# The entry of a last 3x3 convolution: where a row buffer lies, who fills it, and when the other path's result is added

## The chip, the cores and the metric

The kernel runs on one core of one Trainium2 chip. The metric is the device time in microseconds (us) of one execution. The engines of the core run at the same time, each through its own instructions in order: TensorE (PE) multiplies matrices, VectorE (DVE) and ScalarE (ACT) work on elements, GpSimd (POOL) and SyncE (SP) here mostly issue transfers (DMA). A transfer issued by an engine stands in that engine's order too: if it has to wait for a buffer, all that is behind it on that engine waits as well.

## The reference

Four layers work on an array of 4 images, 256 channels, 64 x 64 pixels. Each layer normalises its input over groups of 8 channels, computes a branch and adds the branch to its input. The branches are an axial attention, a ternary 3x3 convolution, a binary network with two 3x3 convolutions, and a plain 3x3 convolution. The change sits between the third and the fourth.

```
x = x + attention(group_norm(x))
x = x + ternary_conv(group_norm(x))
x = x + binary_net(group_norm(x))       # ends with batch_norm(leaky_relu(conv)) on half of the channels
x = x + conv3x3(group_norm(x), W) + bias
```

In the third branch, the last batch normalisation needs sums over all four images before one of its values can be scaled. Its input is called y here (128 channels for each image), and the scaled result is added to the first 128 channels of x. The fourth layer's group normalisation needs x with that addition.

## The kernel before

All four layers are in one program. The chip's memory next to the engines (SBUF) has 128 partitions; a tile holds one channel in each. Tiles come from pools, and pools that are opened one after the other lie one behind the other in memory. When a stage is closed, the next stage's pools are laid over the same bytes; a tile of the new stage can be written only when the last reader of the bytes below it is done. So the order in which pools are opened decides which work of the old stage a new buffer waits for. The binary network's stage opens the pools `e_x`, `e_p`, `e_j`, `e_s`, `e_x1`, ... from the low end. `e_x` (three buffers) and `e_x1` (one) hold input rows, `e_p` a padded input, `e_j` values that nobody reads, and `e_s` the sums and small vectors, which are in use to the stage's very end. The last convolution's stage opens its pools in the order of a string, "t3 m r01 y t0 c s r10 r11 p0 t1 o t2 r00 u0 p1 u1".

A scheduler orders the instructions of each engine at compile time, by priorities that follow the program's order. `tc.high_priority()` puts a block ahead, and `tc.issue_after(i)` places instructions on the engine of `i` behind it. Once made, the orders are fixed.

The last convolution works by image b, by half t of its 256 input channels, by upper and lower half h of the image, and by half co of the output channels. Its steps, with the lines of the profile:

- `fetch` (L1253): a load on SP of 33 rows of x from the output array `out` into the buffer `r` with t and h in its name.
- `measure` (L1267, L1268): on ScalarE, sum and sum of squares of those rows. `norm` then does a chain of small operations, with a square root on ScalarE (L106).
- `transform`: ScalarE normalises the 33 rows into a padded buffer, `g_pad` (L1321, called the fill). VectorE then forms linear combinations of the rows (L1073 to L1086, 12 operations, into `gtr` and `gtm`) and of the columns (L1095, 4 operations, into `gtc`).
- `chunk(b, h, co)`: TensorE makes nine tiles of products, numbered 0 to 8 (L1113, L1120), in a ring of seven PSUM buffers. For tiles 1, 4 and 6 ScalarE makes two copies (L1137, L1138) out of PSUM, and VectorE goes on with them (L1140, L1144, ... L1179). A PSUM buffer is free for a later tile only then. The result `gc_o` is added into `out` by an accumulating transfer on POOL (L1182); for the last image's lower half the sum is made on VectorE and stored by SP (L1186, L1187).

The third layer's result reaches the fourth in two ways. For image 0, upper channels (t = 0), `first_y` adds the scaled y to the fetched rows on VectorE (L1306, ten operations), with the squares on ScalarE (L1316), as soon as the batch normalisation's scale is known. For all images, `add_y` adds it to `out` itself in four pieces. One piece, called a pass here, is a load of y on SP (L1294, into one of two buffers `gy`), a scaling on ScalarE (L1295) and an accumulating transfer on POOL (L1296). Image 1's passes come first, then those of images 0, 2 and 3, at places that `rest` writes down. `fetch` of an image's t = 0 rows has to wait for the passes of the same pixels.

For image 0, `chunk` begins with the t = 1 products of seven tiles, so that TensorE has work while t = 0 is still being made ready.

Of the kernel before, what the change touches and what calls it, by code (L numbers as in the profile page):

```python
# [12 lines left out]
AF = mybir.ActivationFunctionType  # L13
ALU = mybir.AluOpType
# [5 lines left out]
B = 4  # L20
# [21 lines left out]
def network(ctx: ExitStack, tc, x, wqkv, relm, relt, relw, relv, counts, masks, vecs, rowv, ab, w1, l2w1, l2w2, l3w, mats, out):  # L42
# [725 lines left out]
    def from_scores(general, keep):  # L768
# [331 lines left out]
        def output_rows(ring, cp, op, uw, vs, co, res, out_, bias, name, order):  # L1100


            ms, copies = {}, []

            def product(i, t, first, last):
                k, cs = TILES[i]
                if first:
                    ms[i] = ring.tile([P, 8, 64], F32, name=f"{name}_{i}", tag="conv")
                u1, u2 = uw[t]
                v1, v2 = vs[t]  # L1110
                if cs is None:
                    for dx in range(3):
                        nc.tensor.matmul(  # L1113
                            ms[i], lhsT=u1[:, dx, k // 2, bass.ts(co, P)], rhs=v1[:, k // 2, :, dx : dx + 64],
                            start=(first and dx == 0), stop=(last and dx == 2),
                        )
                else:
                    m = ms[i].rearrange("p q (a w) -> p (q a w)", a=2).rearrange("p (a n) -> p a n", a=2)
                    for a, c in enumerate(cs):
                        nc.tensor.matmul(  # L1120
                            m[:, a], lhsT=u2[:, c, k // 2, bass.ts(co, P)],
                            rhs=v2[:, c, k // 2].rearrange("p q w -> p (q w)"), start=first and a == 0, stop=last and a == 1,
                        )

            def tile_(tag):
                return (cp if tag == "c0" else op).tile([P, 512], F32, name=f"{name}_{tag}", tag=tag)

            def halves(a):
                return a.rearrange("p (a n) -> p a n", a=2)

            def flat(m):
                return m.rearrange("p q w -> p (q w)")

            def columns(i, copied, scratch_):
                pair = halves(flat(ms[i]))
                c2 = halves(copied)
                copies.append(nc.scalar.copy(c2[:, 0], pair[:, 1]).ins)  # L1137
                nc.scalar.mul(c2[:, 1], pair[:, 1], -1.0)  # L1138
                sd = halves(scratch_)
                nc.vector.tensor_tensor(sd, pair[:, 0:1].to_broadcast([P, 2, 256]), c2, ALU.add)  # L1140
                return sd

            def whole(i, sd, dst):
                nc.vector.tensor_tensor(  # L1144
                    dst.rearrange("p (n a) -> p a n", a=2), halves(flat(ms[i])), sd, ALU.add
                )

            o4 = op.tile([P, 8, 4, 64], F32, name=f"{name}_o", tag="o4")
            c0, s0, c1, s1 = (tile_(tag) for tag in ("c0", "s0", "c1", "s1"))
            begun = order[2] if order else 0  # L1150
            if order:
                for i in range(begun):
                    product(i, order[0], True, False)
            for i in range(len(TILES)):
                if i < begun:
                    product(i, order[1], False, True)
                else:
                    product(i, 0, True, False)
                    product(i, 1, False, True)
                c, sm = (c0, s0) if i < 3 else (c1, s1)  # L1160
                if i in (1, 4, 6):
                    sd = columns(i, c, sm)
                elif i in (2, 5, 7):
                    whole(i, sd, c)
                if i == 2:
                    m1 = flat(ms[0])
                    nc.vector.scalar_tensor_tensor(s0, m1, bias, c0, ALU.add, ALU.add)
                    nc.vector.scalar_tensor_tensor(c0, m1, bias, c0, ALU.add, ALU.subtract)
                elif i == 5:
                    m3 = flat(ms[3])  # L1170
                    nc.vector.tensor_tensor(s1, m3, c1, ALU.add)
                    nc.vector.tensor_tensor(c1, m3, c1, ALU.subtract)
                    nc.vector.scalar_tensor_tensor(o4[:, :, 2, :], as_rows(s1), 4.0, as_rows(s0), ALU.mult, ALU.add)
                    nc.vector.tensor_tensor(s0, s0, s1, ALU.add)
                    nc.vector.scalar_tensor_tensor(o4[:, :, 1, :], as_rows(c1), 2.0, as_rows(c0), ALU.mult, ALU.add)
                    nc.vector.scalar_tensor_tensor(c0, c1, 8.0, c0, ALU.mult, ALU.add)
                elif i == 7:
                    nc.vector.tensor_tensor(o4[:, :, 0, :], as_rows(c1), as_rows(s0), ALU.add)
            nc.vector.tensor_tensor(o4[:, :, 3, :], ms[8], as_rows(c0), ALU.add)  # L1179
            of = o4.rearrange("p q r w -> p (q r w)")  # L1180
            if res is None:
                nc.gpsimd.dma_start(out=out_, in_=of, accum_op=ALU.add)  # L1182
            else:
                for half in range(2):
                    cols = bass.ts(half, HW // 4)
                    nc.vector.tensor_tensor(of[:, cols], of[:, cols], res[:, cols], ALU.add)  # L1186
                    nc.sync.dma_start(out=out_[:, cols], in_=of[:, cols])  # L1187
            return copies[0]

        def as_rows(a):  # L1190
            return a.rearrange("p (q w) -> p q w", w=64)
# [16 lines left out]
        def conv_layer(name, ph, layout, own, biases, first):  # L1208
# [78 lines left out]
                        nc.vector.tensor_tensor(nb, nb, rs[:, i : i + 1], ALU.mult)  # L1287
                    norms[b, t] = nb, rs[:, i : i + 1]

            def add_y(b, src, scale, shift):  # L1290
                for k in range(4):
                    cols = bass.ts(k, HW // 4)
                    yk = ps_["y"].tile([P, HW // 4], F32, name=f"{name}y_{b}_{k}", tag="y")
                    nc.sync.dma_start(out=yk, in_=src[b][:, cols])  # L1294
                    nc.scalar.activation(yk, yk, AF.Identity, bias=shift, scale=scale)  # L1295
                    nc.gpsimd.dma_start(out=out[b, 0:P, cols], in_=yk, accum_op=ALU.add)  # L1296
# [21 lines left out]
            def transform(b, t, h, pinned=False):  # L1318

                nb, rs = norms[b, t]  # L1320
                filled[b, t, h] = nc.scalar.activation(  # L1321
                    pads[h][:, 1 - h : 34 - h, 1:65], raws[b, t, h], AF.Identity, bias=nb, scale=rs
                ).ins
                v1 = ps_[f"t{2 * h + t}"].tile([P, 3, 8, 66], F32, name=f"{name}tr_{b}_{t}_{h}", tag="tr")
                v2 = ps_[f"t{2 * h + t}"].tile([P, 4, 3, 8, 32], F32, name=f"{name}tc_{b}_{t}_{h}", tag="tc")
                m = ps_["m"].tile([P, 3, 8, 66], F32, name=f"{name}tm_{b}_{t}_{h}", tag="tm")
                input_rows([(v1 if k % 2 else m)[:, k // 2] for k in range(6)], pads[h], pinned)
                ready[b, t, h] = input_columns(v2, m).ins
                vs[b, t, h] = v1, v2
# [8 lines left out]
            def rest(later):  # L1338
                for b in range(B):
                    more = b + 1 < B  # L1340
                    if b > 0:
                        transform(b, 0, 1)
                    chunk(b, 0, 0, first if b == 0 else None)
                    if b > 0:
                        transform(b, 1, 1)
                    if more:
# [3 lines left out]
                        with tc.issue_after(filled[b, 0, 1]):  # L1350
                            measure(b + 1, 1, 0)
                            if b > 0:
                                measure(b + 1, 0, 0)
                    copy = chunk(b, 0, 1, None)
                    if more:
                        for t in (1, 0):
                            fetch(b + 1, t, 1)
# [2 lines left out]
                        with tc.issue_after(copy if b == 0 else filled[b, 0, 1]):  # L1360
                            if b == 0:
                                measure(b + 1, 0, 0)
                            measure(b + 1, 0, 1)
                            if b == 0:
                                later(0)
                        norm(b + 1, slice(0, 2))
                        transform(b + 1, 0, 0)
                    copy = chunk(b, 1, 0, None)
                    if more:
                        transform(b + 1, 1, 0)  # L1370
                        if b + 2 < B:
                            with tc.issue_after(copy):
                                later(b + 2)
                    chunk(b, 1, 1, None)

            return set_up, load_weights, fetch, measure, norm, load_y, first_y, add_y, transform, rest, filled, got, ready

# [255 lines left out]
        with ExitStack() as ph:  # L1633
            xp3 = pool(ph, "e_x", 3)
            padp = pool(ph, "e_p")
            jp = pool(ph, "e_j")
            sp = pool(ph, "e_s")
            xp1 = pool(ph, "e_x1")
            lp = pool(ph, "e_l")
            yps = {b: pool(ph, f"e_y{b}") for b in (3, 0, 1, 2)}  # L1640
            wp2 = pool(ph, "e_w2")
# [237 lines left out]
        with ExitStack() as ph:  # L1879
# [10 lines left out]
            set_up(0)  # L1890
            load_weights(1, nc.gpsimd)
            transform(0, 1, 0)
            for h in range(2):
                fetch(0, 0, h)
            load_y(y_d)
            with tc.high_priority():
                first_y(sy2)
# [2 lines left out]
                norm(0, slice(0, 1), cy2)  # L1900
                transform(0, 0, 0)
            with tc.issue_after(filled[0, 0, 0]), tc.issue_after(got[0, 0, 0]):
                add_y(1, y_d, sy2, cy2)
            with tc.issue_after(ready[0, 1, 0]):
                set_up(1)
            with tc.issue_after(ends[3, 3]):
                transform(0, 1, 1, True)
            transform(0, 0, 1, True)
            rest(lambda b: add_y(b, y_d, sy2, cy2))
        return lost  # L1910

    lost = from_scores(False, keep)
# [114 lines left out]
```

## Time and profile before

| | us |
|---|---|
| median of 3 runs (lowest to highest) | 2702.37 (2691.62 to 2704.37) |
| profiled execution | 2695.66 |
| its span, from the first to the last instruction | 2693.9 |
| busy in the span: TensorE | 2323.6 (86%) |
| busy in the span: VectorE | 1977.6 (73%) |
| busy in the span: ScalarE | 1299.7 (48%) |
| busy in the span: GpSimd | 167.8 (6%) |

Busy shares are averages over four very different layers. The last convolution takes only the last 470 us of the span, from 2222 us on, and the change touches its first stretch. Times in the text are from the start of the span, so that every row can be found on the same axis. In a timeline row the first number is the start, the second the duration, and the brackets at the end give the idle time of that engine just before the row and what ended it.

### The profile page before, as it was taken

What the parts mean: (1) busy time and instruction counts of PE and PEld (TensorE: products, weight loads), DVE (VectorE), ACT (ScalarE), POOL (GpSimd) and SP (SyncE); (2) the same over time, 40 slices, a digit from 0 to 9 for tenths busy, and PEclk for the clock granted to TensorE, in tenths of its full rate; (3) what the DMA queues carried; (4) which work ended last, traced back from release to release, by engine and by line L of the source; (5) the groups of instructions that cost most, each with busy time, mean ns of one, the idle gap of its engine ahead of it and who ended that gap; (6) DMA issues with size and microseconds to landing.
All of it is one profiled execution on the core that took longest, in us unless ns stands there. A gap on an engine that the chain in (4) does not pass through costs nothing. (4 is left out here: it accounts for less than half of the span.)

```text
span 2693.9 us, 78726 instructions
## 1 busy us (share of the span) xinstructions
PE 2323.6 (86%) x34816; PEld 1620.9 (60%) x34816; DVE 1977.6 (73%) x3326; ACT 1299.7 (48%) x2114; POOL 167.8 (6%) x285
## 2 busy tenths in 40 slices
PE   7999888888998788878884999998887887899998
PEld 4656655556666566667663777776444444566665
DVE  6766787888876466666667989986677787688884
ACT  3556354555555654454434655553445753433210
POOL 0000100000000100000000011111000010100000
PEclk9999899999999789989896999999988997999999
DMA  6866476667666887777777666525655775746221
GB/s 234 269 194 196 127 196 183 169 155 202 177 156 146 251 276 252 255 245 257 249 237 255 225 206 226 181 110 193 160 152 170 237 263 150 160 108 148 42 47 49
DMA packets 284832, 505.64 MB, mean 188 GB/s; under 512 B 32896, under 2 KB 149248, under 8 KB 270784
## 3 DMA queue, kind: packets, MB, share of 16 engines
q1 hardware_dynamic: 214336, 347.46, 42.3%
q0 software_dynamic: 21888, 94.32, 13.8%
q10 hardware_dynamic: 48256, 58.73, 6.2%
q8 instruction: 275, 4.51, 0.7%
q14 instruction: 77, 0.63, 0.1%
HBM read 270.45 MB, written 229.97 MB: 186 GB/s over the span
## 5 line engine op out<-in xcount | busy, mean ns | idle before, releaser
L515 DVE STREAM_TRANSPOSE t<-pd 128x1024 f32<-128x1024 f32 x256 | 304.4, 1227 | 84.0 <-PE pd L508 83.1
L508 PE MATMUL pd<-rm,qb 64*32 64x256 f32 x8192 | 310.7, 390 | 48.8 <-DVE t L515 34.6
L1613 PE MATMUL pc<-e_tr,e_k 128*64 128x512 bf16 x2304 | 273.7, 399 | 59.5 <-DVE e_tr L1602 27.9
L535 ACT ACTIVATE o<-pq 128x512 f32<-128x512 f32 x256 | 150.5, 593 | 280.6 <-PE pq L529 280.6
L1113 PE MATMUL gc<-gtr,g_u 128*128 128x512 f32 x576 | 262.6, 608 | 12.8 <-DVE gtr L1077 5.4
L1613 PEld LDWEIGHTS <-e_k 128*64 128x64 bf16 x2304 | 155.6, 114 | 175.6 <-issue 73.9
L508 PEld LDWEIGHTS pd<-rm,qb 64*32 64x32 f32 x8192 | 171.5, 108 | 143.9 <-DVE t L515 60.5
L1509 PE MATMUL dc<-dh,d_u 128*128 128x512 f32 x768 | 230.9, 412 | 23.8 <-ACT dh L1486 21.1
L940 ACT ACTIVATE pt<-pt,sm 128x512 f32<-128x512 f32 x256 | 162.3, 709 | 167.6 <-DVE pt L910 167.6
L1509 PE MATMUL dc<-dl,d_u 128*128 128x512 f32 x768 | 226.5, 405 | 0.9 <-DVE dl L1487 0.7
L1113 PEld LDWEIGHTS gc<-gtr,g_u 128*128 128x128 f32 x576 | 111.2, 195 | 139.2 <-issue 121.3
L529 PEld LDWEIGHTS pq<-t,t 64*64 64x64 f32 x8192 | 143.8, 136 | 83.9 <-issue 74.7
L529 PE MATMUL pq<-t,t 64*64 64x64 f32 x8192 | 165.4, 224 | 26.9 <-issue 25.4
L1120 PE MATMUL gc<-gtc,g_u 128*128 128x256 f32 x768 | 177.5, 388 | 11.3 <-DVE gc_s L1140 7.3
L1509 PEld LDWEIGHTS dc<-dh,d_u 128*128 128x128 f32 x768 | 147.3, 193 | 64.5 <-ACT dh L1486 22.6
L1120 PEld LDWEIGHTS gc<-gtc,g_u 128*128 128x128 f32 x768 | 148.6, 194 | 49.3 <-issue 13.7
L1509 PEld LDWEIGHTS dc<-dl,d_u 128*128 128x128 f32 x768 | 144.8, 190 | 41.9 <-DVE dl L1487 3.4
L910 DVE TENSOR_TENSOR pt<-e_False,si_False 128x1024 f32<-128x1024 f32 x123 | 145.6, 1214 | 25.8 <-PE e_False L898 22.2
L898 PE MATMUL e_False<-qc_False,rw 32*128 32x256 f32 x984 | 124.1, 462 | 31.8 <-DVE pt L910 15.5
L541 ACT ACTIVATE sq<-o 128x1024 bf16<-128x1024 f32 x128 | 135.3, 1057 | 3.9
L291 PE MATMUL po<-xg,wt 128*128 128x512 f32 x256 | 121.0, 612 | 5.3 <-DVE st L298 3.7
L1003 PE MATMUL pe_False<-pt,ve 128*32 128x64 f32 x4096 | 90.8, 243 | 37.9 <-issue 33.1
(415 smaller groups left out, 3913.3 us busy)
## 6 DMA issues: line engine op xcount, KB each, us to landing
si_False<-qk_d SPq DMA_DIRECT2D x64, 1024.0 KB
qk_d<-o SPq DMA_DIRECT2D x496, 128.0 KB
x<-x_d SPq DMA_DIRECT2D x32, 1056.0 KB
gr<-out SPq DMA_DIRECT2D x16, 1056.0 KB
xa<-in_x SPq DMA_DIRECT2D x16, 1024.0 KB
vt_d<-vs ACTq DMA_DIRECT2D x32, 512.0 KB
q_d<-qs SPq DMA_DIRECT2D x64, 256.0 KB
qb<-q_d SPq DMA_DIRECT2D x128, 128.0 KB
```

Source lines behind the costliest of these rows:

```text
L508: nc.tensor.matmul(pds[t][32 * c : 32 * c + 32, m].rearrange("p j k -> p (j k)"), lhsT=q[rows, 2 * (gp % 2) + g, a, 32 * nb : 32 * nb + 32 ...
L515: nc.vector.transpose(ts[t][:, :, 32 * jh : 32 * jh + 32].rearrange("p a j b -> p j a b"), pds[t].rearrange("p m j k -> p j m k"),)
L529: nc.tensor.matmul(ps[nb][64 * g : 64 * g + 64, m, :], lhsT=ts[1][rows, n // 2, :, n % 2], rhs=ts[0][rows, n // 2, :, n % 2], start=True, ...
L535: nc.scalar.activation(o[:, :, n : n + 8, :], ps[nb].rearrange("p n (a b) -> p a n b", b=2), AF.Copy, accum_out=acc[:, nb, gp, col : col + 1],
L541: nc.scalar.activation(junk, part, AF.Square, accum_out=acc[:, 2, gp, col : col + 1])
L898: nc.tensor.matmul(rows_of_e[x_][:, :, :, par], lhsT=rw[rows, 63 - i : 127 - i].rearrange("p j r -> p (j r)"), rhs=q[rows, :, par, k % 2, ...
L910: nc.vector.tensor_tensor(dst, e, src, ALU.add)
L940: nc.scalar.activation(s, s, AF.Exp, scale=s2q[:, gp : gp + 1])
L1113: nc.tensor.matmul(ms[i], lhsT=u1[:, dx, k // 2, bass.ts(co, P)], rhs=v1[:, k // 2, :, dx : dx + 64], start=(first and dx == 0), stop=(las ...
L1120: nc.tensor.matmul(m[:, a], lhsT=u2[:, c, k // 2, bass.ts(co, P)], rhs=v2[:, c, k // 2].rearrange("p q w -> p (q w)"), start=first and a = ...
L1509: nc.tensor.matmul(at[k], lhsT=u[t][:, dx, k, bass.ts(co, P)], rhs=v[:, k, :, dx : dx + 64], start=(first and p_ == 0 and dx == 0), stop=( ...
L1613: nc.tensor.matmul(m[64 * g : 64 * g + 64], lhsT=parts[:, g, i, k, dx, :], rhs=vs[g][:, k, 8 * (q % 2) : 8 * (q % 2) + 8, dx : dx + 64], s ...
```

## The change

It has three parts.

1. The pool `e_x1` is opened right behind `e_p`, so `e_j` and `e_s` come after it. The buffer `r01` then lies over `e_x`, `e_p` and `e_x1`. Image 0's t = 0 loads get a high priority.
2. Image 0's first fill at t = 0, h = 0 is divided: ScalarE fills the first 17 rows, VectorE the other 16.
3. The passes are placed anew. Image 1's third and fourth pass run behind the copies of tile 1 and of tile 4 in the first chunk. The passes of images 2, 3 and 0, in this order, go in pairs: two behind the first copies of `chunk(b, 1, 0)` and two behind those of `chunk(b, 1, 1)`, for b = 0, 1 and 2. Image 0's passes thereby move from image 0's own chunks to image 2's.

```
             def columns(i, copied, scratch_):
...
-                copies.append(nc.scalar.copy(c2[:, 0], pair[:, 1]).ins)
-                nc.scalar.mul(c2[:, 1], pair[:, 1], -1.0)
+                nc.scalar.copy(c2[:, 0], pair[:, 1])
+                copies.append(nc.scalar.mul(c2[:, 1], pair[:, 1], -1.0).ins)
...
-            return copies[0]
+            return copies
...
-            def add_y(b, src, scale, shift):
-                for k in range(4):
+            def add_y(b, pieces, src, scale, shift):
+                for k in pieces:
...
             def transform(b, t, h, pinned=False):
...
+                inner = pads[h][:, 1 - h : 34 - h, 1:65]
+                n = 17 if b == t == h == 0 else 33
                 filled[b, t, h] = nc.scalar.activation(
-                    pads[h][:, 1 - h : 34 - h, 1:65], raws[b, t, h], AF.Identity, bias=nb, scale=rs
+                    inner[:, 0:n], raws[b, t, h][:, 0:n], AF.Identity, bias=nb, scale=rs
                 ).ins
+                if n < 33:
+                    nc.vector.tensor_scalar(inner[:, n:33], raws[b, t, h][:, n:33], rs, nb, ALU.mult, ALU.add)
...
             def rest(later):
...
-                    chunk(b, 0, 0, first if b == 0 else None)
+                    copies = chunk(b, 0, 0, first if b == 0 else None)
+                    if b == 0:
+                        for k in (2, 3):
+                            with tc.issue_after(copies[k - 2]):
+                                later(1, (k,))
...
-                            if b == 0:
-                                later(0)
...
-                        if b + 2 < B:
-                            with tc.issue_after(copy):
-                                later(b + 2)
-                    chunk(b, 1, 1, None)
+                        with tc.issue_after(copy):
+                            later((b + 2) % B, (0, 1))
+                    copy = chunk(b, 1, 1, None)[0]
+                    if more:
+                        with tc.issue_after(copy):
+                            later((b + 2) % B, (2, 3))
...
             xp3 = pool(ph, "e_x", 3)
             padp = pool(ph, "e_p")
+            xp1 = pool(ph, "e_x1")
             jp = pool(ph, "e_j")
             sp = pool(ph, "e_s")
-            xp1 = pool(ph, "e_x1")
...
             transform(0, 1, 0)
-            for h in range(2):
-                fetch(0, 0, h)
+            with tc.high_priority():
+                for h in range(2):
+                    fetch(0, 0, h)
...
-                add_y(1, y_d, sy2, cy2)
+                add_y(1, (0, 1), y_d, sy2, cy2)
```

More of the change, by code (lines that the diff above doesn't have):

```diff
@@ L1353, in rest @@
                                 measure(b + 1, 0, 0)
-                    copy = chunk(b, 0, 1, None)
+                    copy = chunk(b, 0, 1, None)[0]
                     if more:
@@ L1363, in rest @@
                             measure(b + 1, 0, 1)
-                            if b == 0:
-                                later(0)
                         norm(b + 1, slice(0, 2))
                         transform(b + 1, 0, 0)
-                    copy = chunk(b, 1, 0, None)
+                    copy = chunk(b, 1, 0, None)[0]
                     if more:
                         transform(b + 1, 1, 0)
-                        if b + 2 < B:
-                            with tc.issue_after(copy):
-                                later(b + 2)
-                    chunk(b, 1, 1, None)
+                        with tc.issue_after(copy):
[4 more added lines that the diff above has]
+                            later((b + 2) % B, (2, 3))
             return set_up, load_weights, fetch, measure, norm, load_y, first_y, add_y, transform, rest, filled, got, ready
@@ L1908, in from_scores @@
             transform(0, 0, 1, True)
-            rest(lambda b: add_y(b, y_d, sy2, cy2))
+            rest(lambda b, pieces: add_y(b, pieces, y_d, sy2, cy2))
         return lost
```

## The prediction

> **What bounds the kernel now.** I read the chain of waits first, from its end, then each engine's timeline in the stretch where the chain leaves TensorE, then the SP queue's waits.
>
> ```profile
> ## 4 chain that ended last, share of the span: by engine, by line
> PE 11%; issue 1%; DMA 1%; DVE 1%; ACT 0%; POOL 0%; POOLq 0%; DVEq 0%; ACTq 0%; SPq 0%
> ...
> 2390.23 3.65 PE gc L1120 x8
> 2393.88 10.30 PE gc L1113 x24
> ...
> 2679.13 5.16 PE gc L1113 x12
> ```
>
> From 2393.88 to 2684.29 us the chain is TensorE without a hole: 25.81 us for each chunk (10.30 + 3.45 + 5.15 + 6.91). Nothing changed there can gain, unless a hole is made. Before that TensorE waits, and all that it waits less ends the kernel sooner:
>
> ```profile
> 2249.55 6.58 PE L1113 MATMUL gc<-gtr,g_u 128*128 128x512 f32 x10 [5.43 <-DVE gtr L1077]
> ...
> 2265.26 3.78 PE L1120 MATMUL gc<-gtc,g_u 128*128 128x256 f32 x8 [3.43 <-DVE gc_s L1140]
> ...
> 2293.36 8.86 PE L1120 MATMUL gc<-gtc,g_u 128*128 128x256 f32 x32 [3.73 <-DVE gc_o L1179]
> ...
> 2329.61 1.99 PE L1120 MATMUL gc<-gtc,g_u 128*128 128x256 f32 x8 [1.60 <-DVE gc_s L1140]
> ...
> 2339.97 8.31 PE L1113 MATMUL gc<-gtr,g_u 128*128 128x512 f32 x12 [3.10 <-DVE gc_c L1168]
> ...
> 2390.23 3.65 PE L1120 MATMUL gc<-gtc,g_u 128*128 128x256 f32 x8 [2.31 <-DVE gc_s L1140]
> ```
>
> Each wait is for VectorE. What VectorE itself waits for stands in brackets in its own timeline, and ScalarE's timeline gives the cause behind it:
>
> ```profile
> 2237.14 0.95 DVE L1306 SCALAR_TENSOR_TENSOR gr<-g_y,sm,gr 128x64 f32<-128x64 f32 x2 [7.31 <-DMA gr<-out]
> 2247.43 0.71 DVE L1073 SCALAR_TENSOR_TENSOR gtr<-g_pad 128x528 f32<-128x528 f32 x1 [2.22 <-ACT g_pad L1321]
> 2264.51 0.69 DVE L1140 TENSOR_TENSOR gc_s<-gc,gc_c 128x512 f32<-128x512 f32 x1 [4.85 <-ACT gc_c L1138]
> 2323.63 0.17 DVE L108 RECIPROCAL sm<-sm 128x2 f32<-128x2 f32 x1 [12.47 <-ACT sm L106]
> ```
>
> ```profile
> 2259.84 1.24 ACT L1295 ACTIVATE gy<-gy,sm,sm 128x1024 f32<-128x1024 f32 x1 [10.19 <-DMA gy<-y_d]
> 2320.71 1.24 ACT L1295 ACTIVATE gy<-gy,sm,sm 128x1024 f32<-128x1024 f32 x1 [13.76 <-DMA gy<-y_d]
> 2365.61 1.92 ACT L1267 ACTIVATE g_pad<-gr 128x2048 f32<-128x2048 f32 x1 [3.85 <-DMA gr<-out]
> ```
>
> So there are three faults: rows that land late (7.31), a long fill (2.22), and passes of y (L1295) at which ScalarE's in-order queue stands waiting for a load, with the copies or the square root that VectorE needs behind them.
>
> **Part 1, the rows' buffer and load.** The SP row "2228.23 1.80 SPq L1253 x2" and the SP wait "SPq L1253 <- DVE sm L138: 1.0" show the load of image 0's lower rows issued at about 2229.7, when the buffer e_s that it lies over was last read. It landed at 2237.14. By sizes, r01 occupies bytes 24960 to 33408 of a partition (t3 18624, m 6336 below it): now over e_x's end, e_p, e_j and e_s; after, over e_x's end, e_p and e_x1 (29856 to 38304). The last users there are image 3's: the DMA L1712 issued at 2156.37 or at 2167.39 at latest, landing 9.2 us later (DMA issue rows). So the load can go at about 2177 and lands, at the 7.4 us it took before (2229.7 to 2237.1), near 2185. It is needed at 2229. In SP's order it now stands before image 0's upper rows, but those wait for the matmuls until 2202.78 anyway. SP moves too: image 1's lower t=1 rows now stand before its first two y loads, and wait for the fill that ends at 2228.2. So these loads go at 2228.3 and, because y's second buffer now lies over e_s, about 2232.9, instead of 2203.7 and 2225. A y load took 4.5 us to use (2255.30 to 2259.84), so the second is there at 2237.4; ScalarE wants it at 2240. Cost nothing, cover 2.6 us; if late, ScalarE has 10 us of idle time behind it.
> The early load competes. The Trainium skill ("DMA: Bandwidth & Descriptors", "Issuing engines are not separate DMA queues") says that all queues' transfers share the same 16 engines, so a load put into a full stretch is paid by the others. The windows view has a DMA share of 0.87 at 2160 to 2180 and 0.78 to 2200. By the row alone, room for it costs nothing; by the rule, 1056 KB at about 300 GB/s delays the weights g_u by 3.5 us. They are issued until 2179.3, land 15.8 us later, and are first used at 2222.4: 27 us of cover. I take zero.
> VectorE then runs its ten L1306 without a stop: gain 7.3.
>
> **Part 2, the divided fill.** Fill is on the path: ScalarE 2245.24, VectorE 2247.43. 2112 elements take 2.15 us, 1024 take 1.24 (L1295, same form), so 1088 take 1.29: 0.86 less. VectorE's new half (128x1024) has its nearest row in L283, 128x512 f32 in 0.54; twice that is 1.08, still inside 1.29. Gain 0.86 (bounds 0 if VectorE needs 2.1, and 1.1). Parts 1 and 2: **8.2 us**, TensorE starts t=0 at 2241.3.
>
> **Part 3, the passes spread.** *Image 1's third and fourth pass.* Tile 1's products end at 2258.7, yet its copies (L1137) ran at 2263.84, behind the fourth pass. After, only two passes, whose data are there, precede them: shifted by 8.2, products end 2250.5, copies end 2251.2, and L1140 starts at 2251.2 instead of 2264.51, **13.3 earlier, so 5.1 on top of 8.2**. From there VectorE is busy without a hole to 2298, hence it sets TensorE's pace and the 13.3 carries through if its inputs keep up. The third pass, still 11.3 us behind the first (its buffer needs the first's accumulation to land, 7.7, and a load), runs at 2251.6; the copies for tile 4 behind it are done by 2253.6, wanted at 2264.7. The fourth runs by 2255.7; the fill behind it waits for L1086 until 2259.9 anyway. The wait of 3.73 (L1179 behind a whole transform) stays. So does VectorE's 1.21 for DMA out<-gc_o at 2303.7; two passes less before it (2 x 1.13) only make it longer.
> *Image 0's four passes*, whose loads held ScalarE 13.76 us before the square root at 2323.41: they move to image 2's last chunks, with no successor. The root can follow L105 (2310.99, less 13.3) at once, so image 1's transforms start 25 us earlier, when TensorE is 13.3 earlier: 6.6 us behind that chunk's start. In image 2's instance it is 5.5 (2424.95 to 2430.43), where TensorE did not wait. Waits of 1.60 and 3.10 go.
> *Image 2's passes* leave the norm's stretch: two run behind the copies of chunk (0,1,0), two behind those of (0,1,1). In POOL's queue the outputs of (0,0,1) and (0,1,0) now stand before them; the first is issued with VectorE's L1179 (2309.7, less 13.3), the pass follows at 2304, so neither waits for the other. The 2.31 at 2390 depends on the load of image 2's upper rows behind them, see rivals.
> Slow matmuls after a wait also count. The rows show 1.99 for 8 half matmuls, 8.31 for 12 and 3.65 for 8, where the chain's rate is 1.73, 5.15 and 1.73: 0.25 + 3.15 + 1.9 = 5.3. The skill ("TensorE: Matmul & The Clock Gate", Part 1) ties half speed to a free-running window of about 3.4 us, and warns that the cold count varies by run. Waits alone give 7.0; with the rows' slow matmuls 12.3. The granted clock there was 0.87 (2328 to 2354) against 1.00 afterwards, so I take the rows, and keep 7.0 for the range.
>
> Sum: 8.2 + 5.1 + 12.3 = 25.6. New holes: for images 2 and 3 the third pass is a chunk later. Chunk (0,1,1)'s first copies come 33.4 us after (0,1,0)'s start (2424.84 to 2458.23, image 2's instance), the third pass's DMA 2 us later. Rows landed between 15.1 us (7.7 + 7.4) and 19.0 us (2447.53 to 2466.56) after that DMA. Two ScalarE operations on them (4.0) precede tile 6's copies, VectorE then needs 13.1 us (2376.37 to 2389.49) to the next chunk's first L1140, and TensorE can run 19.0 us into that chunk. At 15.1 it does not wait; at 19.0 it waits 1.3 plus 1.9 of slow clock, twice: 0 to 6.4. I take 2. **Net 23.6.** All of it is in one profiled execution of 2695.66 us (span 2693.9), which gives 2672. That run was 6.7 under the median 2702.37; the four runs shown average 2698.5, so I forecast 2675.
>
> **The rivals.**
> A, as summed: 2660 to 2685.
> B, only the entry gains (8 to 10): ScalarE's waits for y are moved, not removed; a late third pass or VectorE's order takes back the rest. For it: VectorE is busy 21.01 of 26 us at 2250 to 2276. Against: it idles 12.47 us at 2323. Time 2689.
> C, slower: the split passes hold image 2's and 3's rows in SP's queue, where they stand behind two y loads and a row load. From 17.9 us after the third pass's DMA each microsecond is paid at both image changes. 28.8 us cancels the gain ((25.6 / 2) - 1.9 + 17.9), 36 us makes it 14 slower: 2712. Against: 17.8 and 19.0 seen, with the same accumulations about.
> D, the load is not early, so the change does not do what it says (another reader of its bytes, or a head of SP's queue that waits): 7.3 is lost, 16.3 is left: 2682.
>
> **How the numbers follow.** A 0.78, B 0.12, C 0.06, D 0.04. About 0.5% (13.5 us) is what measurement can tell from no change. A is faster nearly always (0.76 of its 0.78), B a quarter of the time, D a third: faster 0.80, same 0.14, slower 0.06. The range takes A with its bounds (waits alone: 18; all and no new holes: 26), the spread of runs (6 either way) and B: 2660 to 2697.
>
> **What would show it.** No wait of VectorE at L1306 for gr<-out; L1321 at image 0 about 1.3; a TensorE start of t=0 near 2241 (same span origin); no ScalarE wait over 3 us before L106; no TensorE wait at the places of 2265, 2329 and 2340. I am wrong if L1137 stands behind L1295 again with a DMA as releaser, or TensorE shows new waits at the image changes, 100 us apart.

## The result and the profile after

| | before | after |
|---|---|---|
| median (lowest to highest), 4 runs each | 2703.37 (2691.62 to 2714.49) | 2674.73 (2666.06 to 2681.64) |
| ratio of the times, 95% interval | | 0.99 (0.9866 to 0.9934) |
| the same in a later comparison, 11 and 6 runs | 2708.26 | 2681.30, ratio 0.9907 (0.9884 to 0.9930) |
| profiled execution, its span | 2695.66, 2693.9 | 2681.64, 2679.8 |
| first product of the last convolution | 2222.41 | 2233.98 |
| from there to the end of the span ("the stage") | 471.5 | 445.8 |
| the stage in a second profiled execution | 471.8 | 444.8 |

The change makes the kernel about 1% faster: 27 to 29 us by the medians, 26.4 by the means of the two stages. The forecast was 2675.

The spans of the two profiles differ by only 14.1, because in after's profile everything ahead of the stage took 11.6 longer. One kernel's executions differ by more than that: in the second execution of before the stage began at 2240.09, 17.7 later than in the first, and in the kernels below it began at 2227.4 to 2240.5. So from here on a place is given as the time since the stage's first product ("at 18.2"), and kernels are compared by the length of the stage.

TensorE's timeline of after: the rows of the stage with a wait of over 0.3 in brackets, up to the end of the span.

```profile
2233.98 4.54 PE L1113 MATMUL gc<-gtr,g_u 128*128 128x512 f32 x6 [3.71 <-DVE pc_o L1633]
2246.20 0.38 PE L115 MATMUL pst<-sm,mt 128*128 128x1 f32 x2 [0.78 <-DVE sm L1276]
...
2252.17 5.99 PE L1113 MATMUL gc<-gtr,g_u 128*128 128x512 f32 x10 [4.57 <-DVE gtr L1077]
2258.98 0.70 PE L1120 MATMUL gc<-gtc,g_u 128*128 128x256 f32 x2 [0.83 <-DVE gtc L1095]
...
2281.85 5.42 PE L1113 MATMUL gc<-gtr,g_u 128*128 128x512 f32 x12 [1.67 <-DVE gc_c L1172]
2291.01 7.17 PE L1120 MATMUL gc<-gtc,g_u 128*128 128x256 f32 x32 [3.74 <-DVE gc_o L1179]
...
2304.97 0.38 PE L115 MATMUL pst<-sm,mt 128*128 128x2 f32 x2 [1.64 <-DVE sm L1196]
2308.36 0.38 PE L125 MATMUL pst<-sm,mt 128*128 128x2 f32 x2 [1.18 <-DVE sm L117]
```

After 2309 no row has a wait. The three waits of before at 2329, 2339 and 2390 have no counterpart, nor has the one for L1140 at 2265. The t = 0 products start at 2252.17, that is at 18.19; before it was 27.14. The wait of 3.74 for L1179 has stayed. Two have grown: the one for L1172 from 0.52 to 1.67, and that of the norm's small products from 0.60 to 1.64 + 1.18.

VectorE's timeline of after, the rows at the same places as those shown of before:

```profile
2238.17 0.75 DVE L1306 SCALAR_TENSOR_TENSOR gr<-g_y,sm,gr 128x512 f32<-128x512 f32 x1
...
2248.71 0.81 DVE L1327 TENSOR_SCALAR g_pad<-gr,sm,sm 128x1024 f32<-128x1024 f32 x1
2250.04 0.71 DVE L1073 SCALAR_TENSOR_TENSOR gtr<-g_pad 128x528 f32<-128x528 f32 x1 [0.52 <-ACT g_pad L1323]
...
2262.19 0.68 DVE L1140 TENSOR_TENSOR gc_s<-gc,gc_c 128x512 f32<-128x512 f32 x1
...
2302.15 0.69 DVE L1173 SCALAR_TENSOR_TENSOR gc_o<-gc_s,gc_s 128x512 f32<-128x512 f32 x1 [3.00 <-DMA out<-gc_o]
2309.87 0.17 DVE L108 RECIPROCAL sm<-sm 128x2 f32<-128x2 f32 x1 [0.27 <-ACT sm L106]
```

The 7.31 for the rows is gone, the 2.22 at the fill is 0.52, L1140 follows other work without a gap, and the square root (L106) holds VectorE for 0.27 instead of 12.47. The wait for the transfer of the first chunk's output grew from 1.21 to 3.00. SP's and ScalarE's timelines give the causes:

```profile
2192.90 47.24 SPq L1253 DMA_DIRECT2D gr<-out  x4
```

```profile
2248.71 1.30 ACT L1323 ACTIVATE g_pad<-gr,sm,sm 128x1088 f32<-128x1088 f32 x1 [0.43 <-DVE sm L1287]
2249.91 2.36 ACT L1295 ACTIVATE gy<-gy,sm,sm 128x1024 f32<-128x1024 f32 x2
2261.46 0.37 ACT L1137 COPY gc_c<-gc 128x256 f32<-128x256 f32 x1 [9.19 <-PE gc L1120]
...
2309.63 0.20 ACT L106 ACTIVATE sm<-sm 128x2 f32<-128x2 f32 x1 [4.24 <-DVE sm L105]
...
2356.39 1.92 ACT L1267 ACTIVATE g_pad<-gr 128x2048 f32<-128x2048 f32 x1 [6.88 <-DMA gr<-out]
```

The load of the lower rows is the first of four in the SP row, 48 us ahead of its use at 2240.9. The copies (L1137) wait for TensorE and no longer stand behind a pass, and the root waits only for VectorE's own L105. Image 2's upper rows keep ScalarE waiting 6.88 at the image change, but no wait of TensorE follows there.

### The profile page after: what moved, and what is told of

The parts are those of the page before. It is cut to its first block, busy times and chain, and to the rows that moved or that the text cites. A ratio compares the mean times of both kernels' runs of the same rounds, so it can differ in the third digit from the quotient of the medians.

```text
span 2679.8 us, 78728 instructions
## 1 busy us (share of the span) xinstructions
PE 2325.8 (87%) x34816; PEld 1624.1 (61%) x34816; DVE 1978.3 (74%) x3327; ACT 1298.8 (48%) x2114; POOL 167.9 (6%) x285
## 4 chain that ended last, share of the span: by engine, by line
PE 35%; issue 10%; DMA 9%; DVE 6%; ACT 4%; POOL 0%; SPq 0%; DVEq 0%; ACTq 0%; POOLq 0%
PE dc L1517 13%; PE gc L1113 8%; PE gc L1120 5%; DMA at_d<-o_False 3%; PE e_False L898 2%; PE pr_False L969 2%; PE den_False L951 2%; DMA x<-x_d 2%; PE pe_False L1003 2%; DMA out<-x 2%; DVE pt L910 1%; DMA qc_False<-q_d 1%; PE pa_False L978 1%; DMA a<-at_d 1%; DVE o_False L987 1%
## 5 line engine op out<-in xcount | busy, mean ns | idle before, releaser
L1517 PE MATMUL dc<-dh,d_u 128*128 128x512 f32 x768 | 231.3, 412 | 23.6 <-ACT dh L1494 20.9
L1120 PE MATMUL gc<-gtc,g_u 128*128 128x256 f32 x768 | 171.6, 379 | 4.6 <-DVE gc_o L1179 3.7
L1120 PEld LDWEIGHTS gc<-gtc,g_u 128*128 128x128 f32 x768 | 145.5, 190 | 40.6 <-issue 13.8
L910 DVE TENSOR_TENSOR pt<-e_False,si_False 128x1024 f32<-128x1024 f32 x123 | 145.6, 1215 | 28.6 <-PE e_False L898 25.6
L898 PE MATMUL e_False<-qc_False,rw 32*128 32x256 f32 x984 | 129.9, 488 | 26.8 <-DVE pt L910 13.9
```

Source lines behind the costliest of these rows:

```text
L898: nc.tensor.matmul(rows_of_e[x_][:, :, :, par], lhsT=rw[rows, 63 - i : 127 - i].rearrange("p j r -> p (j r)"), rhs=q[rows, :, par, k % 2, ...
L910: nc.vector.tensor_tensor(dst, e, src, ALU.add)
L1120: nc.tensor.matmul(m[:, a], lhsT=u2[:, c, k // 2, bass.ts(co, P)], rhs=v2[:, c, k // 2].rearrange("p q w -> p (q w)"), start=first and a = ...
L1517: nc.tensor.matmul(at[k], lhsT=u[t][:, dx, k, bass.ts(co, P)], rhs=v[:, k, :, dx : dx + 64], start=(first and p_ == 0 and dx == 0), stop=( ...
```

## The experiments

| kernel | stage, us | against | median, us (before in the same comparison) | ratio to before, 95% |
|---|---|---|---|---|
| before, again | 471.8 | | 2713.77, one run | |
| part 1 alone | 459.4 | before −12.1 | 2695.58 (2697.31) | 0.998 (0.9954 to 1.0007) |
| part 3 alone | 453.9 | before −17.6 | 2685.19 (2697.31) | 0.9933 (0.9906 to 0.9960) |
| image 0's passes back before the root | 452.3 | after +6.5 | 2686.25 (2697.31) | 0.9933 (0.9904 to 0.9963) |
| image 1's passes back before the copies | 450.9 | after +5.1 | 2682.76 (2697.31) | 0.9929 (0.9896 to 0.9961) |
| whole fill | 445.8 | after 0.0 | 2688.11, one run | |
| late passes | 445.8 | after 0.0 | 2679.32 (2700.51) | 0.9913 (0.9881 to 0.9944) |
| transform behind the chunk | 438.2 | after −7.6 | 2671.64 (2700.51) | 0.9889 (0.9848 to 0.9930) |
| after, again | 444.8 | | 2681.30 (2708.26) | 0.9907 (0.9884 to 0.9930) |
| transform behind the chunk, again | 438.3 | | 2674.64 (2708.26) | 0.9887 (0.9863 to 0.9910) |

**Part 1 alone.**

```
             padp = pool(ph, "e_p")
+            xp1 = pool(ph, "e_x1")
             jp = pool(ph, "e_j")
             sp = pool(ph, "e_s")
-            xp1 = pool(ph, "e_x1")
```

> The kernel before with one edit: the pool e_x1 opened behind e_p, no other line. The stage, from the first matmul of the last convolution (L1113) to the end of the span, took 471.5 us before and 445.8 after. Theory A (the terms of the prediction's sum are separate): the early load alone takes away VectorE's 7.31 at L1306 and nothing else, so the stage is 464.2, TensorE's t = 0 products start 7.3 sooner after the stage's start, the 4.85 of L1140 and the 12.47 of L108 stay, the time is 0.27% under before. Rival B (ScalarE's waits for y take the gain back): products start 7.3 sooner, but the third and fourth pass stand at the same time as before, the wait at L1140 grows from 4.85 to about 12, and the stage is 469 to 471.5. Rival D (the load still waits for e_s or for something at the head of SP's queue): the 7.31 stays and the stage is 471.

The stage is 12.1 shorter. The 7.31 is gone, so rival D falls. The priority of the loads isn't in this kernel, so the place of the pool is enough for that. This run's rival B falls too: the wait at L1140 is 4.17, not 12. TensorE's timeline of this kernel:

```profile
2254.30 6.45 PE L1113 MATMUL gc<-gtr,g_u 128*128 128x512 f32 x10 [5.43 <-DVE gtr L1077]
...
2333.42 1.99 PE L1120 MATMUL gc<-gtc,g_u 128*128 128x256 f32 x8 [1.37 <-DVE gc_s L1140]
...
2343.78 6.94 PE L1113 MATMUL gc<-gtr,g_u 128*128 128x512 f32 x12 [3.10 <-DVE gc_c L1168]
...
2392.42 1.99 PE L1120 MATMUL gc<-gtc,g_u 128*128 128x256 f32 x8 [2.11 <-DVE gc_s L1140]
```

The stage began at 2235.02, so the t = 0 products start at 19.28, 7.86 sooner. The other 4.2 are probably not part 1's. The three late waits are all still there, 6.58 together instead of 7.01, and L1140 waits 0.7 less. But the matmuls behind the three took 1.99, 6.94 and 1.99, where before's profile had 1.99, 8.31 and 3.65: 3.0 less, behind waits of nearly the same length. The granted clock was 0.77 over the 6.94 and 0.64 over the 8.31. "Separate terms" was therefore wrong for that term. The change in the times, 0.2%, is not clear of its interval; 12.1 us would be 0.45%, at the interval's edge, and 7.9 us lies well inside.

**Part 3 alone.** The kernel after with parts 1 and 2 undone (the pool's old place, no priority, n = 33 everywhere).

> The kernel before with part 3 alone: the passes of y placed as after, the row buffers and the whole fill as before. Theory A: 5.1 from the tile-1 copies that no longer stand behind two passes, 12.3 from the square root and image 2's passes, 17.4 in all: stage 454, time 0.65% under before; L1306's wait of 7.31 and the 2.22 at the fill stay, L1140's wait of 4.85 goes, TensorE's 1.60, 3.10 and 2.31 go. Waits without slow matmuls would make it 459. Rival B (the waits are moved, not removed): stage 469 to 471.

17.6, where 17.4 was expected. VectorE's rows say that it is the same mechanism:

```profile
2249.96 0.94 DVE L1306 SCALAR_TENSOR_TENSOR gr<-g_y,sm,gr 128x64 f32<-128x64 f32 x2 [7.34 <-DMA gr<-out]
...
2260.24 0.71 DVE L1073 SCALAR_TENSOR_TENSOR gtr<-g_pad 128x528 f32<-128x528 f32 x1 [2.22 <-ACT g_pad L1323]
...
2319.16 0.17 DVE L108 RECIPROCAL sm<-sm 128x2 f32<-128x2 f32 x1 [0.27 <-ACT sm L106]
```

The entry is as before (7.34, 2.22), L1140 has no wait, the root only 0.27, and TensorE has no wait after 2318. This run's rival B falls: two thirds of the change's gain are the passes'.

**Image 0's passes back before the root.**

```
                             measure(b + 1, 0, 1)
+                            if b == 0:
+                                later(0, (0, 1, 2, 3))
...
-                        with tc.issue_after(copy):
-                            later((b + 2) % B, (0, 1))
+                        if b + 2 < B:
+                            with tc.issue_after(copy):
+                                later(b + 2, (0, 1))
...
-                    if more:
+                    if b + 2 < B:
                         with tc.issue_after(copy):
-                            later((b + 2) % B, (2, 3))
+                            later(b + 2, (2, 3))
```

> The kernel after with image 0's four passes put back ahead of the square root of image 1's norm (where they were before); the other passes stay where the change put them. Theory A: VectorE's wait for the root comes back (12.47 before), TensorE waits again at the first chunk of image 1, by 1.60 + 3.10 with 0.25 + 3.15 of slow matmuls: 8.1 in all, stage 453.9; 4.7 (450.5) if the matmuls behind the waits aren't slow. Rival B (the root has so much slack that the passes ahead of it cost nothing, and the gain came from somewhere else): stage 446 to 447.

VectorE's row at the root, and then TensorE's rows:

```profile
2320.58 0.17 DVE L108 RECIPROCAL sm<-sm 128x2 f32<-128x2 f32 x1 [12.04 <-ACT sm L106]
```

```profile
2326.57 1.99 PE L1120 MATMUL gc<-gtc,g_u 128*128 128x256 f32 x8 [1.19 <-DVE gc_s L1140]
...
2336.91 5.42 PE L1113 MATMUL gc<-gtr,g_u 128*128 128x512 f32 x12 [3.09 <-DVE gc_c L1168]
...
2356.45 1.99 PE L1120 MATMUL gc<-gtc,g_u 128*128 128x256 f32 x8 [0.34 <-DVE gc_s L1140]
...
2384.20 1.99 PE L1120 MATMUL gc<-gtc,g_u 128*128 128x256 f32 x8 [1.67 <-DVE gc_s L1140]
```

The stage is 6.5 or 7.5 longer (against the first and the second execution of after), so this run's rival B falls: the wait for the root is on the path. Of theory A the two named waits came (1.19 for the 1.60, 3.09 for the 3.10), but the slow matmuls didn't: 12 took 5.42 behind a wait of 3.09, hardly more than the chain's 5.15. Two waits that A hadn't named came in their place (0.34, 1.67). The second stands where before had 2.31: image 2's rows are loaded late again, behind six loads of y in one SP row (2307.77 to 2342.79), although image 2's own passes are where the change put them.

**Image 1's third and fourth pass back before the copies.**

```
-                    if b == 0:
-                        for k in (2, 3):
-                            with tc.issue_after(copies[k - 2]):
-                                later(1, (k,))
...
-                add_y(1, (0, 1), y_d, sy2, cy2)
+                add_y(1, (0, 1, 2, 3), y_d, sy2, cy2)
```

> The kernel after with image 1's third and fourth pass put back ahead of the copies of tile 1. Theory A: L1137 for tile 1 runs 5.1 us later (behind the fourth pass), VectorE stands before L1140 for some 4.8, and because it has no hole until 2302 this reaches TensorE whole: stage 450.9. Rival B (VectorE's later wait of 3.00 for the output's transfer, and TensorE's ring, take it up): stage 446 to 448.

ScalarE's timeline, and the row of VectorE that waits for it:

```profile
2259.84 1.24 ACT L1295 ACTIVATE gy<-gy,sm,sm 128x1024 f32<-128x1024 f32 x1 [10.74 <-DMA gy<-y_d]
2263.05 1.24 ACT L1295 ACTIVATE gy<-gy,sm,sm 128x1024 f32<-128x1024 f32 x1 [1.97 <-DMA gy<-y_d]
2264.20 0.35 ACT L1137 COPY gc_c<-gc 128x256 f32<-128x256 f32 x1
```

```profile
2264.86 0.69 DVE L1140 TENSOR_TENSOR gc_s<-gc,gc_c 128x512 f32<-128x512 f32 x1 [5.77 <-ACT gc_c L1138]
```

L1140 runs at 34.04 instead of 28.21, and L1179's wait ends 5.84 later. The stage is 5.1 or 6.1 longer, so theory A's 5.1 holds, and this run's rival B (taken up later) falls.

**The fill whole again.** n = 33 for every fill; all else as after.

> The kernel after with the fill of image 0's first t = 0 rows whole again, on ScalarE alone. Theory A: ScalarE 2.15 instead of 1.30, VectorE waits 2.22 and has no 0.81 of its own; the t = 0 products start 0.86 later, stage 446.7. Rival F (the divided fill brings more or less than its own duration, because TensorE's matmuls behind the wait change speed): the start of the products 0.86 later, but the stage elsewhere than 446.2 to 447.2.

```profile
2259.50 7.16 PE L1113 MATMUL gc<-gtr,g_u 128*128 128x512 f32 x10 [5.43 <-DVE gtr L1077]
...
2298.36 8.86 PE L1120 MATMUL gc<-gtc,g_u 128*128 128x256 f32 x32 [3.73 <-DVE gc_o L1179]
```

From a stage begun at 2240.47 the products start at 19.03, 0.84 later than after's 18.19, and the wait for L1179 ends at 57.89, 0.86 later. Yet the stage has after's length. The difference is lost between L1179 and L1173: from the issue of the transfer of gc_o until VectorE goes on it took 7.96 here and 8.75 in after's profile, so L1173 starts at 68.2 in both. The second execution of after tells whether the 8.75 comes back.

**Both kernels again.**

> The kernel before, unchanged, profiled once more: how much of the 471.5 us stage is the same in a second execution. Theory G (the slow matmuls behind TensorE's waits are a state of the clock that differs by execution): the waits of 7.31, 4.85 and 12.47 on VectorE and of 3.10 and 2.31 on TensorE come back within 0.3, but the rows after them (8.31 for 12, 3.65 for 8, 1.99 for 8) do not, and the stage is 466 to 472. Rival H (a wait of a given length always slows the same matmuls, as the prediction's 5.3 took it): the same durations within 0.3 each and a stage of 471 to 472.

> The kernel after, unchanged, once more: 445.8 us for the stage in its first execution, in which the transfer out<-gc_o let VectorE go on 11.14 after L1179 had started the matmuls behind it, against 10.2 to 10.4 in the other kernels. Theory G: this one has 10.2 to 10.4, the waits of 1.64 and 1.18 become some 0.6 together, and the stage is 444.5 to 445.5; beside the kernel without the divided fill (445.8) the 0.86 is then seen again. Rival (the divided fill's 0.86 is taken up by the wait for that transfer): 11 again and 445.8.

After: the transfer took 7.81, the wait of 3.00 is 2.04, the norm's products wait 0.44 and the stage is 444.8, so against this execution the divided fill is worth 1.0, near its 0.86. The long transfer did not come back; why it was long is open. Before: 471.8, with VectorE's waits of 6.96, 4.98 and 12.57. TensorE's late rows:

```profile
2347.05 1.99 PE L1120 MATMUL gc<-gtc,g_u 128*128 128x256 f32 x8 [1.70 <-DVE gc_s L1140]
...
2357.39 6.96 PE L1113 MATMUL gc<-gtr,g_u 128*128 128x512 f32 x12 [3.09 <-DVE gc_c L1168]
...
2379.51 1.99 PE L1120 MATMUL gc<-gtc,g_u 128*128 128x256 f32 x8 [1.38 <-DVE gc_s L1140]
...
2408.25 3.68 PE L1120 MATMUL gc<-gtc,g_u 128*128 128x256 f32 x8 [2.66 <-DVE gc_s L1140]
```

The 8.31 became 6.96 behind the same wait (granted clock 0.77, not 0.64), which speaks for theory G; the 3.65 came back as 3.68, and a wait of 1.38 came in addition. So the total repeated better than its rows.

**Late passes.** Images 2's, 3's and 0's third and fourth pass behind the third pair of copies (tile 6) of `chunk(b, 1, 1)`, not the first.

```
-                    copy = chunk(b, 1, 1, None)[0]
+                    copy = chunk(b, 1, 1, None)[2]
```

> The kernel after with the third and fourth pass of images 2, 3 and 0 behind the copies of tile 6 instead of tile 1 of chunk (b,1,1), some 11 us later. The measurement of the upper rows then stands later in ScalarE's order too, as the scheduler puts it. Rival C's price: rows 14.1 + 11 = 25 us after the old place of the third pass, 7 us over the threshold of 17.9, with 1.9 of slow matmuls 9 us at each of two image changes: stage 464. Theory A without that price (nothing that TensorE needs stands behind the rows until the norm, some 40 us later): stage 446 to 448, no TensorE wait at 2350 to 2370 or 2455 to 2475.

```profile
2349.53 2.37 ACT L1295 ACTIVATE gy<-gy,sm,sm 128x1024 f32<-128x1024 f32 x2
2368.63 1.92 ACT L1267 ACTIVATE g_pad<-gr 128x2048 f32<-128x2048 f32 x1 [16.73 <-DMA gr<-out]
```

```profile
2371.21 0.69 DVE L1140 TENSOR_TENSOR gc_s<-gc,gc_c 128x512 f32<-128x512 f32 x1 [8.32 <-ACT gc_c L1138]
```

```profile
2366.49 7.46 PE L1120 MATMUL gc<-gtc,g_u 128*128 128x256 f32 x32
```

The rows are used at 140.6, 18.2 later than after's 122.4; ScalarE waits 16.73 and VectorE 8.32. TensorE loses only 0.4, and the stage is 445.8, not the 464 of rival C's price. That price was worked out with both measuring operations ahead of tile 6's copies. In this build the scheduler put only one of them (L1267) ahead of the next chunk's first copies. The waiting L1140 ends at 2371.90. TensorE's next half matmul waits for it, starts at 2371.95 and is 0.4 late; that is why the row of 32 takes 7.46 and not the usual 7.07. It stands 19.2 after that chunk's start (2352.74: TensorE's row of 24 products begins at 2347.59, and the first 12, 5.15 us, are the last tile of the chunk ahead). So the limit of 19.0 that the prediction gave TensorE's ring was just met. At the other image change VectorE waited 7.03 and TensorE lost nothing. What lies further past that limit wasn't tried.

**Transform behind the chunk.** The step that stayed in the way, the transform of image 0's lower t = 0 rows, written behind the first chunk.

```
                     copies = chunk(b, 0, 0, first if b == 0 else None)
...
-                    if b > 0:
-                        transform(b, 1, 1)
+                    transform(b, 0 if b == 0 else 1, 1)
...
-            transform(0, 0, 1, True)
```

> The kernel after with one step moved: the transform of image 0's t = 0, h = 1 rows is written behind chunk (0,0,0) and no longer pinned ahead of it; its results are first read at chunk (0,1,0), some 50 us after the stage's products start. What remains of TensorE's waits behind the entry are 1.67 (L1172) and 3.74 (L1179), both behind that transform on VectorE, and 1.64 + 1.18 behind the norm's sums, which stand behind VectorE's wait of 3.00 for the transfer out<-gc_o. Theory A (VectorE's order sets TensorE's pace up to 2309): L1179 comes 5.4 sooner, the transfer starts sooner, and the stage is 445.8 less 5.4 to 8.2: 437.6 to 440.4. Rival E (VectorE is busy without a hole from 2250 to 2302, so its work is the bound and the order can't help: the transform's 12 us are missing later, at chunk (0,0,1) or (0,1,0)): stage 444 to 447.

> The kernel with the transform of image 0's lower t = 0 rows behind chunk (0,0,0), unchanged, once more beside the kernel after on the same chip: stage 438 to 439 again, 7 less than after; the time 0.2 to 0.3% under that of after, which the intervals may not tell apart.

TensorE has one wait of over 0.2 behind the start of this kernel's t = 0 products (first profile):

```profile
2299.41 7.13 PE L1113 MATMUL gc<-gtr,g_u 128*128 128x512 f32 x16 [1.84 <-DVE gc_c L1144]
```

1.67, 3.74 and the norm's 1.64 + 1.18 are gone, and VectorE's L1173 has no wait for the transfer. The stage is 438.2 and 438.3, inside theory A's 437.6 to 440.4; rival E falls. VectorE was busy without a hole, and its order still cost time: it worked on what is wanted only 50 us later. By the stage this version beats both kernels, by 7 and 33 us. Against before, the times show it (0.9887, 0.9863 to 0.9910); against after, the intervals overlap.

## Why the prediction was right

| step | predicted | measured |
|---|---|---|
| part 1: VectorE's wait for the rows | 7.3 gone | gone; sums of the norm (L1195) 7.65 sooner |
| the early load costs nothing | 0; by the rule, weights 3.5 later | 0: the weights land 3 later, yet the first product waits 3.71 for the layer ahead, before 3.75 |
| part 2: the fill | 0.86, VectorE's half at most 1.08 | products 0.84 sooner, half 0.81 |
| start of t = 0 products | 8.2 sooner | 8.95 sooner |
| L1140 of tile 1 | 13.3 sooner | 13.89 sooner; undone: 5.1 to 6.1 lost |
| wait of L1179 behind the transform | stays at 3.73 | 3.74 |
| image 1's transforms | 25 sooner | 25.3 sooner |
| waits of 1.60, 3.10, 2.31 | 7.0 gone | gone |
| slow matmuls behind them | 5.3 gone | gone here, but not a constant |
| new holes at the image changes | 2 (0 to 6.4) | 0 |
| sum | 25.6, net 23.6 | 25.7; 26.4 by two executions each |

Theory A holds: each part does what it was said to do, where it was said, and B, C and D fall. The early load went a little later than worked out: at 2192.90, which is 2181.3 on before's axis and not 2177. It waited for an output transfer that was issued at 2179.00 and took 13.8, where 9.2 had been taken. With some 40 us in hand that costs nothing. These are the windows of 20 us around it, before and after (last columns: clock, DMA share, GB/s):

```profile
2180.00:2200.00 20.00, 19.02 (x169) 10.87 (x167) 11.55 (x34) 12.21 (x17) 0.00 (x0) 1.00 0.78 299
```

```profile
2191.00:2211.00 20.00, 18.86 (x167) 10.76 (x165) 11.41 (x36) 12.79 (x17) 0.00 (x0) 1.00 0.92 352
```

The share rose from 0.78 to 0.92, and TensorE's and VectorE's busy times (the second and the fourth number of the row, 19.02 and 18.86, 11.55 and 11.41) are nearly the same. The rule of the shared engines did bite: the last of the first six transfers of weights (g_u) landed 18.9 after its issue, before 15.8. It was 18.2 to 18.9 in the eight profiles with the early load that show it, and 15.7 to 15.8 in the three without. That is the delay that the prediction put at 3.5 by the rule, and the cover made it free: the weights were there at 2209.05 and first used at 2233.98.

Four terms were off in size.

- The entry: 0.75 more. With the rows there, TensorE has been idle 0.78 instead of 8.44 ahead of the norm's small products; they take 0.38 for two instead of 0.59, which makes the norm 0.45 shorter, and the squares are 0.27 less late.
- The new holes: the 2 us allowed for them was too much. Image 2's rows were used 14.06 after the third pass's DMA, less than the 15.1 that had been taken as the best case, and when they were used 18.2 later (late passes), TensorE lost 0.4 at one image change and nothing at the other.
- The wait for gc_o's transfer: "only longer" was right (3.00 and 2.04), but it isn't free. The norm's sums stand behind it on VectorE, and TensorE stood 2.8 for them in one execution and 0.44 in the other. Not all of that is the transfer's: the sums (L1195) came 0.96 later in the first, and the 32 half matmuls ahead took 7.17 there and 8.86 in the second, so TensorE was ready 1.7 sooner.
- The slow matmuls: taken as 5.3 from one execution. By the same reckoning (the row less the time that as many matmuls take in the chain without holes) it was 4.3 in the second execution of before (0.26 + 1.81 + 0.26 + 1.95), 2.3 in part 1 alone and 1.05 with image 0's passes put back. It is a term with a spread of 1 to 5.

That last term is also why the parts don't add up: 12.1 + 17.6 + 0.9 = 30.6. Part 1's run happened to have 3.0 less of the slow matmuls and 1.1 less of waits which part 3 removes altogether; 30.6 − 4.1 = 26.5 fits the 26.4.

So the net of 23.6 came out 2.8 too low, most of it the 2 us for holes that did not come. The step from the profile's own time to the median, the last of the sum, moved 2672 to 2675; it took before's typical time for 2698.5, and the comparisons gave medians of 2697.31 to 2708.26. In the first comparison (2703.37) that level was 4.9 too low and the gain 2.8 too low; the two errors have opposite signs in the time. So it is partly luck that the measured 2674.73 lies 0.3 from the forecast.

## What to carry to other kernels

Where an engine works its queue in order, look at what stands ahead of the instruction that the bound engine waits for. Here a load into the right bytes and passes moved behind others' work gave 26 us, without one instruction less. Ask of each early step when its result is first read: a transform pinned 50 us ahead of its use cost 7 us. Compare a stage's length from its own first instruction: what comes ahead of it varied by 18 us between executions, and the gain that was to be seen was 26.

## What the runs showed of the hardware

- A wait of one length is followed by matmuls of different speed. Behind the wait of 3.73 to 3.74 for L1179, 32 half matmuls took 7.17 in after's profile, 8.86 in its second execution and 9.94 with the late passes, with 6.91 in the chain; the granted clock over these rows was 1.00, 0.80 and 0.71. Behind 3.09 to 3.10, 12 took 5.42, 6.94, 6.96 and 8.31, at 1.00, 0.77, 0.77 and 0.64. The Trainium skill ("TensorE: Matmul & The Clock Gate", Part 1) says that the window of the clock's throttle is free-running and warns against fitting to a cold count. The spread agrees with the warning; where the window lay, no run shows. The prediction, which quoted it, put the 5.3 of one execution into its sum and left the spread to its range.
- Where VectorE waited for it, the accumulating transfer of the first chunk (1024 KB) took 7.8 to 8.1 from its issue to VectorE's next step in nine profiles, and 8.75 in the tenth. That one transfer, 0.79 longer, hid the 0.86 of the divided fill.
